# Routed pages of the last six blocks: stored whole by SyncE and gathered later, in place of a scatter by Pool

## The chip, the cores and the metric

The kernel runs on one core of a Trainium2 chip. The metric is the device time of one execution in microseconds (us); lower is better. All data are fp32 (the one-hot matrices of the routing are bf16).

## The reference

A two-layer graph network on 8192 tokens (128 graphs of 64 nodes) of width D = 256. Each layer adds a graph convolution and then a mixture of experts.

```python
# layer 0
n = layernorm(x)
h = silu(rmsnorm((eps * n + adj @ n) @ W1 + b1))         # 256 -> 1024
x = x + (h @ W2 + b2)                                    # 1024 -> 256
n = layernorm(x)
top, idx = top_k(n @ gate_w.T, 6)                        # 6 of 64 experts per token
s = softmax(top)
lattice = sum_k s[k] * (n @ lattice_weights[idx[k]])     # 256 x 256 per expert
x = x + layernorm(n + lattice @ out_w.T + out_b)
# layer 1
n = layernorm(x)
x = x + (n + relu((adj @ n) @ W_rel + b_rel + n @ W_root))
n = layernorm(x)
x = x + sum over top 2 of 8 experts of softmax weight * (relu(n @ W1[e] + b1) @ W2[e] + b2)
```

## The kernel before

The tokens are worked on in 32 blocks (NB) of 256 tokens, two tiles of 128 partitions each. There are four stages.

**The first fused pass** goes over the blocks in a software pipeline (`staggered`, a list of steps with lags, so that a step of the loop holds pieces of eight blocks or so). It computes layer 0's convolution, the gate's logits, the top six experts and each token's row in the table of that expert. Pool sends each tile's rows, six times per token, into a DRAM table `r0x` with an indirect transfer (`Router.send`, L334). A row is 258 words: 256 of the token, its target row in the answers (token x 6 + rank), and its softmax weight. `Router.places` works out the rows with 64-wide one-hot products on DVE, `Router.books` keeps the experts' chunks of the table. After the last block `Router.page_table` computes, on DVE, where each page of 128 rows starts and which expert it belongs to. The lattice weights, 16 MB, are loaded into SBUF piece by piece; the last pieces go to where this pass had its weights and scratch (L829 to L832).

**The expert pass** runs over pages. Twelve early pages, known before the table is complete, go first (`fetch_early`, `flip_early`, `apply_early`). Then come 202 pairs of pages: SP fetches a page with a row number read from the page table (L480); PE turns it (L903), ACT copies it (L905), PE multiplies it with the expert's matrix, chosen by a register (L918), DVE scales it by the softmax weights in place (L922), and Pool scatters the 128 rows to the answers `r0y` with an indirect transfer, each row to its own target (`Router.reply`, L341). `px` has 22 buffers of a pair. In the first 64 pairs ACT also issues one transfer each of a page of filler rows to the end of each expert's rows (`fill_end`, L193): a filler row's target lies outside of the answers, and its reply is dropped. More pages than the 404 run only under a condition on the number of pages (`needed`).

**The second fused pass** loads each block's six answers per token with two plain transfers of 768 KB by SP (`load_y`, L974), adds them up while turning them (`mixture`, L994), and computes out_proj, the layer norms, layer 1's convolution, its gate, and the sends of its rows (two per token) by Pool to the table `r1x`.

**The eight experts** of layer 1 run over 69 pages of 256 rows.

The order of PE, DVE and ACT is the order in which the code issues instructions (`manual_schedule`). The orders of SP's and Pool's instructions are chosen by a scheduler. Where steps share a tile or a DRAM tensor the framework adds semaphore waits; `alone` and `declare_no_dep` say which transfers need not wait for each other. The weights `lat` are one tile, so a matmul with a matrix chosen by a register waits for all loads into it.

Of the kernel before, what the change touches and what calls it, by code (L numbers as in the profile page):

```python
# [78 lines left out]
class Router:  # L79
# [15 lines left out]
    def __init__(self, tc, pool, small, dram, n, D, E, K, T, pg, S, epoch, name, R, total=None, like=None):  # L95
# [4 lines left out]
        self.pages = K * n // pg + E - 1  # L100

        self.likely_pages = K * n // pg + E // 2 + max(E // 8, 1)
        self.full_pages = -(-(K * n - E * (pg - 1)) // pg)
# [26 lines left out]
        if self.J > 1:  # L130
            self.nth = self.iota([P, self.J, E], [[1, self.J], [0, E]], 0, "nth")
            self.end, self.delta, self.alloc, self.none = (
                pool.tile([P, E], F32, name=name + x) for x in ("endrow", "delta", "alloc", "none"))
            self.used = pool.tile([P, 1], F32, name=name + "used")
            for t, v in ((self.delta, 0), (self.alloc, 1), (self.used, E), (self.none, 1)):
                nc.gpsimd.memset(t, float(v))
            nc.vector.tensor_scalar(self.end, self.base, float(S), None, op0=ALU.add)
# [3 lines left out]
        if total is None:  # L141
            self.answer = dram.tile([n * K, D], F32, name=name + "y")
            nc.gpsimd.iota(fill_to, pattern=[[0, pg // P]], base=n * K, channel_multiplier=0)
# [4 lines left out]
        self.taken = None  # L148
        self.fill(nc.sync, self.spare)
# [20 lines left out]

    def iota(self, shape, pattern, m, name):
        t = self.pool.tile(shape, F32, name=self.name + name)
        i = self.small.tile([P, 384], I32, name="iota", bufs=1)[:, :t.free_size()]
# [24 lines left out]
    def choose(self, logits):  # L198
# [7 lines left out]
        which = self.small.tile([P, T, K], F32, name=n + "which")  # L206
# [100 lines left out]
    def places(self, b, hot):  # L307
# [8 lines left out]
        nc.vector.tensor_add(place, pos, run)  # L316
        if self.J > 1:
# [30 lines left out]

    def add(self, i, x, y):
# [8 lines left out]
    def page_table(self, scratch):  # L358
# [10 lines left out]

        wide = lambda t, k, m: t.unsqueeze(k).to_broadcast([P, 4, m])  # L370
# [13 lines left out]
        v.tensor_scalar(full, cnt, 1.0 / pg, (pg - 1.0) / (2 * pg), op0=ALU.mult, op1=ALU.subtract)  # L384
        v.tensor_scalar(full, full, MAGIC, None, op0=ALU.add)
        v.tensor_scalar(full, full, -MAGIC, None, op0=ALU.add)
        v.scalar_tensor_tensor(part, full, -float(pg), cnt, op0=ALU.mult, op1=ALU.add)
        v.tensor_scalar(part, part, 0.0, None, op0=ALU.is_gt)
        if self.taken is not None:
            v.tensor_sub(full, full, self.taken)  # L390
        v.tensor_scalar(first, full, float(self.R), None, op0=ALU.min)
        v.tensor_sub(rest, full, first)
        v.tensor_tensor_scan(cum, num, self.zero, 0.0, op0=ALU.add, op1=ALU.add)
        self.total_pages = self.pool.tile([P, 1], I32, name=n + "total")
        if self.seen is None:
# [13 lines left out]
        start = small([J, 4], "pstart")  # L409
        self.tab = self.pool.tile([P, 2, 4], I32, name=n + "tab")  # L410
# [11 lines left out]
        v.scalar_tensor_tensor(nth, two, float(self.R), nth, op0=ALU.mult, op1=ALU.add)  # L422
        v.tensor_mul(le[:, :, :E], ate, wide(full, 1, E))
        v.tensor_reduce(no, le[:, :, :E], op=ALU.add, axis=AX.X)
        v.tensor_mul(no, no, three)
        v.tensor_add(nth, nth, no)
        if self.taken is not None:
            v.tensor_mul(le[:, :, :E], ate, wide(self.taken, 1, E))
            v.tensor_reduce(no, le[:, :, :E], op=ALU.add, axis=AX.X)
            v.tensor_add(nth, nth, no)  # L430
        for j in range(J):
            v.tensor_mul(le[:, :, :E], ate, wide(self.map[:, j, :], 1, E))
            v.tensor_reduce(start[:, j, :], le[:, :, :E], op=ALU.add, axis=AX.X)
        v.scalar_tensor_tensor(row, nth, float(pg), start[:, 0, :], op0=ALU.mult, op1=ALU.add)
        for j in range(1, J):
            v.tensor_sub(no, start[:, j, :], start[:, j - 1, :])
            v.scalar_tensor_tensor(no, nth, float(j * self.S // pg), no, op0=ALU.is_ge, op1=ALU.mult)
            v.tensor_add(row, row, no)
        v.tensor_scalar(no, kind, float(V), None, op0=ALU.is_lt)
        v.tensor_scalar(row, row, float(self.spare), None, op0=ALU.subtract)  # L440
        v.tensor_mul(row, row, no)
        v.tensor_scalar(self.tab[:, 0, :], row, float(self.spare), None, op0=ALU.add)
        v.tensor_scalar(self.tab[:, 1, :], exp, float(E - 1), None, op0=ALU.min)

    def fill_end(self, e):

        if e % 4 == 0:
            _, self.ends = self.nc.values_load_multi_w_load_instructions(
                self.last[0:1, e:e + 4], engines=[ENG.Activation], min_val=0, max_val=self.spare - self.pg,
                skip_runtime_bounds_check_because="the rows of an expert end in its chunk")  # L450
        self.fill(self.nc.scalar, self.ends[e % 4])

    def load(self, what, i, engine):
# [3 lines left out]
            self.tab[i // 4:i // 4 + 1, what, :], engines=[engine], min_val=0, max_val=top,  # L457
# [3 lines left out]
    def needed(self, n):  # L461

        _, (v,) = self.nc.values_load_multi_w_load_instructions(
            self.total_pages[0:1, :], min_val=0, max_val=self.pages,
# [14 lines left out]
    def fetch(self, i, row, out):  # L479
        d = self.nc.sync.dma_start(out=out, in_=self.table[ds(row, self.pg), :].rearrange("(t p) d -> p t d", p=P))  # L480
        if i < self.full_pages:
# [13 lines left out]
def two_layer_gnn_moe_kernel(ctx: ExitStack, tc: tile.TileContext, a: dict, out: bass.AP):  # L495
# [16 lines left out]
    READY = 5  # L512
    LOOK = 20
# [57 lines left out]
    def load_adjacency(b):  # L571
        at = adjacency[b % 4]
# [4 lines left out]

    x1_dram = [dram.tile([C, D], F32, name=f"x1_{b}") for b in range(NB)]
    xn1_dram = [dram.tile([C, D], F32, name=f"xn1_{b}") for b in range(NB)]
    r0 = Router(tc, const, small, dram, N, D, E0, K0, T, P, 14 * P, 4, "r0", 3)  # L580
# [23 lines left out]
    with tc.tile_pool(name="c0", bufs=1) as c0, \  # L604
# [12 lines left out]
        def load0(b):  # L617
# [3 lines left out]
            B["at"] = load_adjacency(b)  # L621
# [133 lines left out]
        def choose(b):  # L755
            B = blocks[b]
            B["top"], B["hot"] = r0.choose(pg)
# [8 lines left out]
        def place(b):  # L766
# [4 lines left out]
            if b == READY - 1:  # L771
                r0.look_back()
            if b == LOOK:
# [8 lines left out]
        def load_lattice(b):  # L782
            n = free[0] // 16
            if 8 <= b < 24:

                nc.vector.memset(lat[:1, (b - 8) * n, 0, :1], 0.0)
                nc.sync.dma_start(out=lat[:, (b - 8) * n:(b - 7) * n], in_=lat_w[:, (b - 8) * n:(b - 7) * n])

# [36 lines left out]
            (1, load_lattice),  # L825
        ))
        r0.page_table(sq.rearrange("p c n -> p (c n)"))
        n = free[0] // 16
        nc.sync.dma_start(out=lat[:, 16 * n:free[0]], in_=lat_w[:, 16 * n:free[0]])  # L829
        for i in (0, 5, 2, 3, 1, 6, 4):  # L830
            e = E0 - EB * (i + 1)
            nc.sync.dma_start(out=lat[:, e:e + EB], in_=lat_w[:, e:e + EB])  # L832
# [3 lines left out]
    with tc.tile_pool(name="e0", bufs=1, reuse_waits="tile") as ex, \  # L836
# [39 lines left out]
        staggered(EARLY // 2, ((-2, flip_early), (0, apply_early)))  # L876


    with tc.tile_pool(name="wx0", bufs=3, reuse_waits="tile") as wx, \
            tc.tile_pool(name="pt1", bufs=4, space=PSUM, reuse_waits="tile") as pt_pool, \  # L880
            tc.tile_pool(name="py1", bufs=4, space=PSUM, reuse_waits="tile") as py_pool:
        npair = (r0.pages + 1) // 2
        pairs = [dict() for _ in range(npair)]
        regs = {}
        ring = [wx.tile([P, KD, C], F32, name="pxT", bufs=5)]

        def fetch(j):
            Q = pairs[j]
            Q["px"] = px = wx.tile([P, 2, W], F32, name="px", bufs=22)
            for q in range(2):  # L890
                i = 2 * j + q
                if i % 4 == 0:
                    regs["row"] = r0.load(0, i, ENG.SP)
                if i < r0.pages:
                    r0.fetch(i, regs["row"][i % 4], px[:, q:q + 1, :])

        def flip(j):
            Q = pairs[j]
            pt = pt_pool.tile([P, KD, C], F32, name="pt")
            n = min(2, r0.pages - 2 * j)  # L900
            for q in range(n):
                for k in range(KD):
                    nc.tensor.transpose(pt[:, k, ts(q, P)], Q["px"][:, q, ts(k, P)], ident)  # L903
# [375 lines left out]
```

## Time and profile before

| | |
|---|---|
| median of 14 runs | 2308.92 us (2291.88 to 2319.18) |
| the profiled execution's own time | 2309.56 us |
| its span in the profile | 2307.8 us |
| mean granted TensorE clock | 0.948 |
| PE busy in the span | 1997.1 us, 87% |
| Pool busy | 1158.0 us, 50% |
| DVE busy | 1196.0 us, 52% |
| sends of the first pass (L334) on Pool | 384, 1039 ns each |
| replies (L341) on Pool | 404, 972 ns each |

The profile is of one execution. Busy time counts the instructions that compute, and on Pool the indirect transfers, which its processors work out themselves; transfers that SP and ACT issue are not busy time. A line of a group has the source line, the engine, the operation, output and input, the count, then busy time, mean duration in ns of one, and the idle time of that engine just before these instructions with what ended most of it. A line of waits has the waiting engine, tile and line, what it waited for, and then total us, times, and the longest. "issue" is a wait for nothing that the profile shows.

### The profile page before, as it was taken

Reading aid. Unit: us, or ns where it says so; the run is one execution under the profiler, and the core shown is the slowest. Engines: PE = TensorE matmul, PEld = TensorE weight load, DVE = VectorE, ACT = ScalarE, POOL = GpSimd, SP = SyncE. Lnnn points to the kernel's source line nnn. Section 1 sums busy time; section 2 is a strip of 40 time slices with the busy share of each in tenths; the row PEclk is TensorE's granted clock in tenths of the full one; section 3 lists DMA queues with packets and bytes.
Section 4 is the critical chain, followed back from the end, with each engine's and each line's share of the span. In section 5 each row is a group of like instructions: output and inputs, shape, how many; then the busy total and the mean of one; then the engine's idle time right before and its main releaser. Section 6 shows DMA issues by size and latency. Waiting matters only on the chain. (4 is left out here: it accounts for less than half of the span.)

```text
span 2307.8 us, 37214 instructions
## 1 busy us (share of the span) xinstructions
PE 1997.1 (87%) x10516; PEld 1714.3 (74%) x10516; DVE 1196.0 (52%) x4205; ACT 1012.8 (44%) x2033; POOL 1158.0 (50%) x1134
## 2 busy tenths in 40 slices
PE   7988888888884687887878887999997999999997
PEld 6877777777663466666766766888886888888886
DVE  5878778778786222222223224999997222222221
ACT  5867666667661121211111113666664333333332
POOL 0455555556556566666666661333334343444443
PEclk9999999999996899899998898999998999999998
DMA  3323444444345787755555527998872776676674
GB/s 110 99 100 130 138 139 136 138 139 132 106 161 186 217 244 211 220 175 171 178 175 173 154 66 276 324 318 273 277 237 78 171 173 153 166 165 165 165 165 97
DMA packets 282560, 397.91 MB, mean 172 GB/s; under 512 B 56024, under 2 KB 236392, under 8 KB 282352
## 3 DMA queue, kind: packets, MB, share of 16 engines
q1 hardware_dynamic: 202880, 246.61, 36.2%
q0 software_dynamic: 64416, 136.14, 19.8%
q10 hardware_dynamic: 15056, 12.69, 1.7%
q8 instruction: 94, 1.54, 0.3%
q14 instruction: 114, 0.93, 0.1%
HBM read 222.84 MB, written 176.64 MB: 173 GB/s over the span
## 5 line engine op out<-in xcount | busy, mean ns | idle before, releaser
L334 POOL DMA_INDIRECT r0x<-xs,r0row x384 | 398.9, 1039 | 349.1 <-DVE xs L305 145.5
L918 PE MATMUL py<-lat,pxT 128*128 x1616 | 424.5, 409 | 112.2 <-ACT pxT L905 79.6
L341 POOL DMA_INDIRECT r0y<-px x404 | 392.8, 972 | 227.6 <-DVE px L922 109.3
L918 PEld LDWEIGHTS py<-lat,pxT 128*128 128x128 f32 x1616 | 314.8, 205 | 165.8 <-ACT pxT L905 87.7
L922 DVE TENSOR_SCALAR px<-py,px 128x256 f32<-128x256 f32 x404 | 170.5, 478 | 449.4 <-PE pt L903 161.8
L351 POOL DMA_INDIRECT out_x<-py_s,px x138 | 214.7, 1556 | 292.9 <-DMA out_x<-py_s,px 211.7
L905 ACT COPY pxT<-pt 128x512 f32<-128x512 f32 x202 | 114.0, 588 | 517.2 <-remote 193.3
L1217 ACT ACTIVATE phid<-ph,pw 128x256 f32<-128x256 f32 x276 | 130.9, 474 | 322.5 <-issue 212.4
L1215 PE MATMUL ph<-pxT,pw 128*128 128x256 f32 x1104 | 251.6, 381 | 0.7 <-ACT pxT L1206 0.7
L1235 PE MATMUL py<-fw,phid 128*128 (+1 forms) x1104 | 249.7, 379 | 0.0
L717 PE MATMUL ps<-lat 128*128 128x256 f32 x1024 | 245.9, 390 | 0.0
L684 PE MATMUL ph<-lat 128*128 128x256 f32 x1024 | 239.3, 392 | 5.9 <-DVE lat L706 2.8
L1215 PEld LDWEIGHTS ph<-pxT,pw 128*128 128x128 f32 x1104 | 211.1, 191 | 30.2 <-ACT pxT L1206 1.1
L334 POOL DMA_INDIRECT r1x<-xs,r1row x128 | 127.3, 994 | 200.2 <-ACT xn3T L1106 51.9
L684 PEld LDWEIGHTS ph<-lat 128*128 128x128 f32 x1024 | 198.0, 196 | 37.2 <-issue 7.8
L1235 PEld LDWEIGHTS py<-fw,phid 128*128 128x128 f32 x1104 | 204.5, 190 | 25.0
L717 PEld LDWEIGHTS ps<-lat 128*128 128x128 f32 x1024 | 198.5, 196 | 26.6
L903 PE MATMUL pt<-ident,px 128*128 128x128 f32 x808 | 132.1, 286 | 15.5 <-DMA px<-r0x 8.2
L903 PEld LDWEIGHTS pt<-ident,px 128*128 128x128 f32 x808 | 108.0, 149 | 42.6 <-issue 19.3
L1229 DVE TENSOR_SCALAR p<-p 128x2 f32<-128x2 f32 x69 | 13.5, 195 | 228.0 <-ACT p L1228 228.0
L687 ACT ACTIVATE lat<-ph,c_L_gnn_b 128x256 f32<-128x256 f32 x256 | 101.0, 472 | 61.9 <-PE ph L684 38.5
L1238 DVE TENSOR_TENSOR py_s<-py,pb 128x512 f32<-128x512 f32 x69 | 47.7, 691 | 153.4 <-PE py L1235 153.3
(303 smaller groups left out, 2980.0 us busy)
## 6 DMA issues: line engine op xcount, KB each, us to landing
px<-r0x SPq DMA_DIRECT2D x404, 129.0 KB
y<-r0y SPq DMA_DIRECT2D x64, 768.0 KB
pw<-in_L_ffn_W1b SPq DMA_DIRECT2D x69, 514.0 KB
px<-r1x SPq DMA_DIRECT2D x69, 258.0 KB
x<-x SPq DMA_DIRECT2D x64, 256.0 KB
pb<-in_L_ffn_b SPq DMA_DIRECT2D x69, 128.0 KB
r0x<-r0filler ACTq DMA_DIRECT2D x64, 129.0 KB
lat<-in_x SPq DMA_DIRECT2D x32, 256.0 KB
```

Of the source, the lines that this page charges most:

```text
L334: i = self.nc.gpsimd.indirect_dma_start(out=self.table[:, :], out_offset=bass.IndirectOffsetOnAxis(ap=row[:, t, k:k + 1], axis=0), in_=xs[ ...
L341: d = self.nc.gpsimd.indirect_dma_start(out=self.answer[:, :], out_offset=bass.IndirectOffsetOnAxis(ap=x[:, self.D:self.D + 1].bitcast(I32 ...
L351: i, d = f"{self.name}add{i}", self.nc.gpsimd.indirect_dma_start(out=self.total[:, :], out_offset=bass.IndirectOffsetOnAxis(ap=x[:, self.D ...
L684: nc.tensor.matmul(ph[:, c, :], lhsT=w1[:, k, ts(2 * j + c, P)], rhs=B["aggT"][:, k, :], start=(k == 0), stop=(k == KD - 1))
L717: nc.tensor.matmul(B["po"][:, t, :], lhsT=B["hT"][:, c, ts(t, P)], rhs=w2[:, c, :], start=False, stop=(t == T - 1 and c == KH - 1))
L903: nc.tensor.transpose(pt[:, k, ts(q, P)], Q["px"][:, q, ts(k, P)], ident)
L905: nc.scalar.copy(xT[:, :, :n * P], pt[:, :, :n * P])
L918: nc.tensor.matmul(py[:, q, :], lhsT=xT[:, k, ts(q, P)], rhs=lat[:, ds(regs["e"][(2 * j + q) % 4], 1), k, :].rearrange("p o d -> p (o d)") ...
L922: nc.vector.tensor_scalar(px[:, q, :D], py[:, q, :], px[:, q, D + 1:D + 2], None, op0=ALU.mult)
L1215: nc.tensor.matmul(ph, lhsT=w[:, k * F1 + c * P:k * F1 + (c + 1) * P], rhs=Q["xT"][:, k, :], start=(k == 0), stop=(k == KD - 1))
L1217: nc.scalar.activation(hid[:, c, :], ph, AF.Relu, bias=w[:, KD * F1 + c:KD * F1 + c + 1], scale=1.0)
L1235: nc.tensor.matmul(py[:, t, :], lhsT=Q["hid"][:, c, ts(t, P)], rhs=fw2[:, ds(e, 1), c, :].rearrange("p o d -> p (o d)"), start=(c == 0), s ...
```

## The change

The tokens' blocks are split into the first 26 ("near") and the last six ("far", `FAR = 6`), and the pages of layer 0's experts with them:

- A page with near rows in it is a near page; a page that holds only far rows is a far page. There are two page tables: `page_table` for the near pages, and a new function `far_table`, issued on DVE after the early pages, for the far ones. The expert pass runs 168 pairs of near pages and 34 pairs of far pages, 404 pages as before; the far pairs are strewn between the near ones from the 40th item on. `px` has 20 buffers of a pair.
- Far pages have no reply on Pool. SP stores them whole, in the order of the page's rows, to a slot of a new DRAM tensor `r0paged` (`Router.store`). Near pages from number 128 on have a reply on Pool and a store on SP, since they may hold far rows too.
- `Router.clear` writes zeros to the slots that no store may reach, with 30 transfers of up to 1 MB on SP in the first fused pass.
- The far blocks keep the experts' numbers (`which`) and the places within the expert (`nth`, five more DVE operations in `places`). `Router.locate` turns them into rows of `r0paged`, with twelve DVE operations for a far block, two per item in 36 items of the expert pass, ahead of the scale.
- In the second fused pass the far blocks are worked on among the near ones (steps 7, 12, 17, 22, 27 and 31), and their answers are fetched by Pool with 12 indirect gathers of 128 rows each, four per step of the loop, instead of by `load_y`.
- The fillers of `fill_end` are issued by SP instead of ACT, three per pair for the first 22 pairs. One of the lattice loads, the last, is issued after `far_table`, whose scratch it overwrites.
- Two more conditions follow the expert pass: one runs further far pairs, one runs stores of the first 128 near pages, where the counts call for it.

The core of the diff, with the new functions:

```diff
+    def store(self, slot, y):
+        d = self.nc.sync.dma_start(out=self.paged[ts(slot, self.pg), :], in_=y)
+        self.alone(d.ins, "store")
+
+    def clear(self, lo, hi):
+        self.nc.sync.dma_start(
+            out=self.paged[lo * self.pg:hi * self.pg, :].rearrange("(s p) d -> p s d", p=P),
+            in_=self.filler[:, 0:1, :self.D].to_broadcast([P, hi - lo, self.D]))
+
+    def locate(self, b, work):
...
+        def find(what):
+            return (lambda: v.tensor_mul(prod, hot, spread(what)),
+                    lambda: v.tensor_reduce(got, prod, op=ALU.add, axis=AX.X))
+        return (
+            lambda: v.tensor_tensor(hot, spread(self.expert), self.whiches[b].unsqueeze(3).to_broadcast([P, T, K, E]),
+                                    op=ALU.is_equal),
+            *find(far),
+            lambda: v.tensor_tensor(prod[:, :, :, 0], nth, got, op=ALU.is_ge),
+            lambda: v.tensor_copy(self.whiches[b], prod[:, :, :, 0]),
+            *find(more),
+            lambda: v.tensor_mul(self.whiches[b], self.whiches[b], got),
+            *find(begin),
+            lambda: v.tensor_add(got, got, self.whiches[b]),
+            lambda: v.tensor_add(at, got, nth),
+        ), at
+
+    def gather(self, at, t, k, y):
+        self.nc.gpsimd.indirect_dma_start(
+            out=y[:, t, k, :], out_offset=None, in_=self.paged[:, :],
+            in_offset=bass.IndirectOffsetOnAxis(ap=at[:, t, k:k + 1], axis=0))
...
     def places(self, b, hot):
...
+        if self.is_far(b):
+            nth = self.nths[b] = self.pool.tile([P, T, K], F32, name=n + f"nth{b}")
+            prod = self.work.tile([P, T, K, E], F32, name=n + "prod", bufs=1)
+            nc.vector.tensor_sub(prod[:, :, 0, :], place, self.base.unsqueeze(1).to_broadcast([P, T, E]))
+            nc.vector.tensor_mul(prod[:, :, 1:, :], hot[:, :, 1:, :],
+                                 prod[:, :, 0:1, :].to_broadcast([P, T, K - 1, E]))
+            nc.vector.tensor_mul(prod[:, :, 0, :], hot[:, :, 0, :], prod[:, :, 0, :])
+            nc.vector.tensor_reduce(nth, prod, op=ALU.add, axis=AX.X)
...
     def fill_end(self, e):
...
-        self.fill(self.nc.scalar, self.ends[e % 4])
+        self.fill(self.nc.sync if self.split else self.nc.scalar, self.ends[e % 4])
...
-        r0.page_table(sq.rearrange("p c n -> p (c n)"))
+        far_table = r0.page_table(sq.rearrange("p c n -> p (c n)"))
...
-        for i in (0, 5, 2, 3, 1, 6, 4):
-            e = E0 - EB * (i + 1)
-            nc.sync.dma_start(out=lat[:, e:e + EB], in_=lat_w[:, e:e + EB])
+        load_back(0, 5, 2, 3, 1, 6)
...
         staggered(EARLY // 2, ((-2, flip_early), (0, apply_early)))
+        far_table()
+        load_back(4)
...
+            def apply(self):
+                if not self.far and not self.again:
+                    for e in range(3 * self.j, min(3 * self.j + 3, E0)):
+                        r0.fill_end(e)
...
+                for f in self.extra:
+                    f()
+                kept = self.far or self.again or self.pages[0] >= r0.sure
+                for q, i in enumerate(self.pages):
+                    nc.vector.tensor_scalar(px[:, q, :D], py[:, q, :], px[:, q, D + 1:D + 2], None, op0=ALU.mult)
+                    if not self.far and not self.again:
+                        r0.reply(i, px[:, q, :], px[:, q, :D])
+                    if kept:
+                        r0.store(i + (r0.slots[0] if self.far else 0), px[:, q, :D])
...
+            staggered(len(items), ((-12, lambda s: items[s].fetch()), (0, lambda s: items[s].apply()),
+                                   (-2, lambda s: flip(items[s], True)), (-3, lambda s: flip(items[s], False))))
...
+        for j, x in enumerate(near(0, mean_pages)):
+            items.append(x)
+            while more and j >= lead and (j - lead + 1) * mean_far >= (mean_far - len(more) + 1) * (mean_pages - lead - 2):
+                items.append(more.pop(0))
...
+        for x in items[lead + 4::2]:
+            if work:
+                x.extra = work.pop(0), *([work.pop(0)] if work else [])
...
+        with tc.If(r0.needed(2 * mean_far, r0.far_total)):
+            run(beyond(mean_far, (r0.far_pages + 1) // 2))
+        with tc.If(r0.needed(0, r0.short)):
+            run([Pair(j, again=True) for j in range(r0.sure // 2)])
...
+        def gather_y(b, lag, i):
+            if b < NB - FAR:
+                return
+            B = blocks[b]
+            if lag == 0 and i == 0:
+                B["y"] = work.tile([P, T, K0, D], F32, name="yg", bufs=1)
+            k = lag * YS + i
+            r0.gather(found[b], k // K0, k % K0, B["y"])
+
         def load_y(b):
+            if b >= NB - FAR:
+                return
...
-        staggered(NB, (
+        gathers = lambda i: tuple((m - 5, lambda b, m=m: gather_y(b, m, i)) for m in range(3))
+        steps = (
...
+        staggered(NB, tuple((lag, f if f is load_w2 else lambda s, f=f: f(order[s])) for lag, f in steps))
```

## The prediction

> **What bounds the kernel now.** I read the table of slices first, to split the span into stages.
>
> ```profile
> PE   7988888888884687887878887999997999999997
> POOL 0455555556556566666666661333334343444443
> PEclk9999999999996899899998898999998999999998
> DMA  3323444444345787755555527998872776676674
> ```
>
> One slice is 57.7 us. Slices 0 to 12 are the fused pass (to about 733 us), slices 13 to 23 the expert pass (first reply 774, last 1394), slices 24 to 30 the second fused pass (to about 1780), the rest the eight experts. The change edits the first three. Pool's digit is highest in the expert pass, 6, but not 9; PE stands at 7 to 8, so neither is full there. Next, the groups of instructions of that pass.
>
> ```profile
> L918 PE MATMUL py<-lat,pxT 128*128 x1616 | 424.5, 409 | 112.2 <-ACT pxT L905 79.6
> L341 POOL DMA_INDIRECT r0y<-px x404 | 392.8, 972 | 227.6 <-DVE px L922 109.3
> L922 DVE TENSOR_SCALAR px<-py,px 128x256 f32<-128x256 f32 x404 | 170.5, 478 | 449.4 <-PE pt L903 161.8
> L905 ACT COPY pxT<-pt 128x512 f32<-128x512 f32 x202 | 114.0, 588 | 517.2 <-remote 193.3
> ```
>
> A reply costs Pool 0.97 us and 0.30 us of issue, 1.276 us. 404 of them are 515 of the 620 us: Pool is 83% taken, and its order has no other work. Whether Pool paces this pass is the question on which the sign hangs, so I asked for the waits between 800 and 1390 us, and for those of SP.
>
> ```profile
> ACT pxT L905 <- remote: 175.3, 36, 10.5
> DVE px L922 <- PE pt L903: 161.8, 35, 8.5
> POOL r0y L341 <- DVE px L922: 105.1, 57, 2.7
> POOL r0y L341 <- issue: 103.7, 322, 1.9
> PE py L918 <- ACT pxT L905: 72.2, 30, 5.9
> ```
> ```profile
> SPq L480 <- DMA r0y<-px: 30.1, 16, 3.4
> ```
>
> Pool waits 105 us for DVE. DVE scales `px` in place, so Pool can hold up PE in one way only: a reply frees its `px` buffer late, SP fetches late, PE finds no page. SP waits for replies 30 us in all, and the fetches of pair j are issued a nearly constant 44 us ahead of its flip from pair 42 on, by the records of L480 and L903. PE never starves for a page. The pace, 2.9 to 3.1 us per pair (flips: pair 60 at 951.1, pair 180 at 1313.8), is set by PE, ACT and DVE: PE's work for a pair takes 2.17 us at full clock, and about every fifth pair a hole of 2.5 to 6 us opens in which ACT's copy and DVE's scale resume together, late (PE stands from 1090.0 to 1095.6; in the hole Pool sends three more replies and then runs dry too). The holes add up to 119 us of the 590. The trace does not name their cause. The windows show what follows from them.
>
> ```profile
> 800.00:850.00 50.00, 43.08 (x219) 36.28 (x219) 14.52 (x34) 9.96 (x17) 30.58 (x32) 0.96 0.88 259
> 1000.00:1050.00 50.00, 39.40 (x185) 33.07 (x186) 13.46 (x32) 9.28 (x17) 31.27 (x34) 0.90 0.57 174
> 1350.00:1400.00 50.00, 35.04 (x164) 29.54 (x162) 12.77 (x30) 6.84 (x12) 29.17 (x30) 0.81 0.30 99
> 1450.00:1500.00 50.00, 50.00 (x345) 45.19 (x346) 45.02 (x206) 32.38 (x69) 18.60 (x22) 1.00 0.96 327
> ```
>
> Columns are the window, its length, busy time of PE, PE weight load, DVE, ACT and Pool with counts, granted clock, DMA share, GB/s. 32 replies pass in the window with a DMA share of 0.88 as in that with 0.57: transfers do not pace the expert pass. In the second fused pass PE is full, 50 of 50, and DMA at 0.96.
>
> **The change, part by part.** The sum is made against the profiled execution, 2309.56 us (span 2307.8); the median of the runs shown is 0.64 lower.
>
> *First fused pass.* Added: 30 transfers on SP that clear some 31 MB, without a wait on compute; DMA share is 0.2 to 0.4 in slices 0 to 10, and 31 MB at the 259 GB/s of the window at 800 are 120 us of a 730 us pass, so they fit, but the first blocks' x loads stand behind some of them on SP. For the six late blocks five more DVE operations each; the two wide ones and the reduction by the rows of the same forms (768 elements, 0.95 us; 640 about 0.85), the rest 0.2: 2.4 us a block. DVE is some 80% busy in a step of 21.2 us, PE 87%, so four of six blocks' share hides. After the last block DVE alone runs `page_table`: eleven operations of 64 elements (0.20 each) and one lookup (0.42 + 0.42) more, 3.2 us, all on the path (L372 to L443 stand alone from 733 to 752.5). I take +4, between 0 and 14.
>
> *Start of the expert pass.* Now the last lattice load (L832) leaves at 752.5 and the first `py` of the main loop starts at 770.3. In the changed order the last megabyte of the lattice waits for `far_table`, which stands on DVE behind the early pages, the last of which DVE ends at 769.9. `far_table` has some 50 operations; priced as in `page_table` (0.42 for 4x64, 0.2 for the small ones, 0.56 a scan), 14.3 us: it ends at 784 or, with the longer table, 787. Then 512 KB pieces land in 3.4 us and 768 KB in 6.6, so the first `py` comes near 790 to 794, 20 to 24 later. Does it come back? Nine pairs are fetched by then, but 56 of the 64 fill transfers, now SP's, stand between the next 25 pairs' fetches. SP issued the dynamic fetches of pairs 6 to 36 at 1.9 us a pair (776 to 836), 0.95 each; a static transfer takes 0.37 to 0.50, 0.95 if it queues like those. So from 787 SP needs 25 x 1.9 = 48 and 56 x 0.4 to 0.95 = 22 to 53 us, and has pair 34 out between 857 and 888. PE, at the old 2.9 us a pair from 792, comes to it near 890: at the worse price just fed, and in no case faster than it was. Nothing comes back. +20, between 8 and 30.
>
> *Replies to stores.* 68 far pages lose their reply: Pool is relieved of 68 x 1.276 = 87 us. By the waits above that frees an engine that waits, so I take 0, between -87 (if Pool were the bound) and 0. Added: 276 stores of 128 KB on SP. From 888 on SP has 168 pairs x 1.9 = 319 us of fetches and 276 x 0.5 to 0.6 = 138 to 166 of stores, and would end near 1345 to 1373; PE, started 20 late at the old pace, fetches its last page near 1355. So SP, idle before, becomes level with PE. But each store waits for a DVE scale, and the next fetches stand behind that wait on SP; with 18 pairs of lead that is covered by some 53 us, less when SP falls back. SP also shows stretches in which each of its instructions takes 0.7 us. I take +5; at 0.95 us a store the stores are 262 us, SP ends at 1469, about 100 late. The 35 MB on the DMA engines are +0.9 us a pair beside 1.7 now, under a pace of 3.0: free. Here the Trainium skill speaks against the idea: its page "DMA: Bandwidth & Descriptors", section "Issuing engines are not separate DMA queues", says that transfers from all issuing engines run on the same 16 DMA engines, and that spreading the issue saves only the sequencer's time. The trace agrees that the sixteen are shared (0.88 at 800 with fills, fetches and replies together), and shows that they do not pace this stage; by the rule alone the swap would gain nothing and cost the added bytes.
>
> *Locating.* 72 DVE operations, seven of 0.95 and five of 0.17 per block, 45 us in all, two per pair on 36 pairs. DVE is busy 13.5 of 50 us here; a step of 3 us has room, but they stand before the scale, so each delays PSUM's release by up to 1.9 us, covered by four `py` buffers. +2, between 0 and 15.
>
> *Tail of the pass.* Two more conditions on every engine. An If costs ACT 1.0 us now (1381.2 to 1382.2), PE 3.7. The stores must land before the far gathers; +3, between 1 and 8. No branch of the three should run: the counts of these inputs stay under their thresholds (335 near pages for 336, 65 far for 68).
>
> *Second fused pass.* 72 gathers of Pool replace 12 of the 64 y loads. Pool's step has four sends, 5.7 us of about 10.9; four gathers at 1.28 make 10.8 in 18 of 32 steps: level with PE. The gathers stand in front of the sends on Pool, whose wait at the end is short. Against this stage's DMA share of 0.96 the bytes are the same. +5, between 0 and 25.
>
> Sum: 4 + 20 + 5 + 0 + 2 + 3 + 5 = +39, so 2348.
>
> **The rivals.** *Pool paces the expert pass after all.* For it: Pool's period, 2.55 us a pair, is above PE's 2.17, its idle time is spread thin, and when PE holds fast Pool's queue grows; the holes of ACT and DVE might come with Pool's descriptor work. Against it: the waits. Then up to 87 us go, and the costs of 39 stay: 2261, between 2255 and 2300. It decides if the pace falls below 2.7 us a pair in the stretch of far pairs. *SP becomes the bound*: stores at 0.95 us, pass three starts near 1469 instead of 1389: +80 and the costs outside, about 2400. It decides if an SP step of two fetches and 1.64 stores passes 3.0 us. *The start is made good and the rest hides*: 2309, no change. *A branch runs*: 34 pairs x 2.95 = +100; the inputs' counts speak against it.
>
> A second rule bears on the holes. After PE stands from 1117.5 to 1123.7 the granted clock is 0.50 for some 4 us: a hole costs more than its length. "TensorE: Matmul & The Clock Gate", section "What's actually happening", has the clock halved after an idle window; fewer holes would thus pay twice, in the rival's favour, which no row here can settle.
>
> **How the numbers follow.** My forecast 0.44, SP as the bound 0.18, Pool as the bound 0.27, all hidden 0.08, a branch 0.03. About 0.3%, 7 us, is what a measurement of this kernel can tell from no change: faster 0.27, same 0.08, slower 0.65. The likeliest case alone runs from 2322 to 2385. The range reaches into both neighbours, to 2262 (most of the Pool case kept) and to 2400, and leaves out half of SP's tail and the branch.
>
> **What would show it.** Right: the first main `py` 15 to 25 us later than 770; pairs at 2.9 to 3.1 us all through the far stretch; Pool's waits for DVE grown by about 87 us; the second fused pass about 390 us as now. Wrong: pairs under 2.7 us after item 40 (Pool did pace), or over 3.2 with SP's queue full and PE waiting on `px` (SP paces); a second fused pass above 410 us with PE waiting on gathered y; a first `py` before 780.

## The result: 5% slower

The changed kernel takes 2434.37 us (median of ten runs), the kernel before 2308.76 us (47 runs): a ratio of 1.054, between 1.051 and 1.057. The profiled execution has a span of 2430.6 us, 122.8 us more than the one before. The experiments below are single executions, each beside one of the kernel before; that took 2306 to 2326 us in the series e1 to e4, e9 to e12 and e13 to e16, but 2057 us in the series e5 to e8, on the chip of e1 to e4 (the other two series ran on two more chips), so that those four are compared with 2057 and with each other alone.

The page of the changed kernel, slices of 60.8 us:

```profile
PE   7988888888843779978778829788889899999997
POOL 0456555556564556655444421444453434444444
PEclk9999999999976889999999969888889899999999
DMA  9964444443363777777777768766763476776665
```

The clearing shows in DMA's first three slices and does not touch PE there. PE's expert pass has two parts, 9 9 7 and then 8 7 7 8. The hole at its end (2) is deeper than before, and the second fused pass, which was 9 throughout, is full of 8. Its groups:

```profile
L370 POOL DMA_INDIRECT r0y<-px x336 | 335.5, 999 | 288.7 <-DVE px L1099 194.8
L1092 PE MATMUL py<-lat,pxT 128*128 x1616 | 411.8, 400 | 52.6 <-issue 21.7
L1099 DVE TENSOR_SCALAR px<-py,px 128x256 f32<-128x256 f32 x404 | 174.1, 479 | 398.4 <-PE py L1092 212.3
L1082 ACT COPY pxT<-pt 128x512 f32<-128x512 f32 x202 | 115.3, 587 | 525.2 <-PE pt L1080 292.3
```

Pool waits for DVE 195 us now (109 before): grown by 86, near the 87 that the prediction named as a sign. By first and last instructions of each stage:

| stretch | before, us | after, us | difference | predicted |
|---|---|---|---|---|
| start to the end of `page_table` | 752.5 | 763.0 | +10.5 | +4 |
| to the first `py` of a pair | 17.8 | 34.9 | +17.1 | +20 |
| to the end of the last scale | 619.6 | 601.8 | -17.8 | +7 |
| to the first transpose of the mixture | 3.9 | 36.3 | +32.4 | +3 |
| to the first matmul of the eight experts | 388.8 | 471.9 | +83.1 | +5 |
| to the end | 525.2 | 522.7 | -2.5 | 0 |

The expert pass got faster and the two stretches behind it, priced at 8 us together, cost 115. The first row varies from run to run where the code is the same (749 to 800 us in the runs of the changed kernel's kind below).

Windows of the three parts of the expert pass (length, busy PE, weight load, DVE, ACT, Pool; clock, DMA share, GB/s), then two lines of the waits from 1040 to 1400 us, of PE and of Pool:

```profile
900.00:1040.00 140.00, 128.10 (x671) 110.14 (x670) 74.23 (x157) 31.20 (x56) 90.64 (x90) 0.96 0.70 210
1040.00:1390.00 350.00, 279.98 (x1322) 216.91 (x1322) 110.46 (x248) 63.80 (x110) 176.06 (x178) 0.96 0.74 229
1390.00:1436.00 46.00, 8.80 (x45) 7.42 (x44) 4.35 (x10) 1.17 (x2) 11.28 (x13) 0.65 0.53 176
```
```profile
POOL r0y L370 <- DVE px L1099: 128.9, 51, 6.6
...
PE pt L1080 <- DMA px<-r0x: 45.5, 49, 2.6
```

From item 36 to 90 an item takes 2.52 us (904.8 to 1040.9) and PE is busy 128 of 140 us. From item 96 the fetches' lead over the flips, up to 13 us until then, is 1 to 3 us, PE waits for `px` 45.5 us (8.2 in the whole kernel before), and an item takes 3.2 us. From 1040 to 1390 SP issues 216 fetches and 214 stores: the slots of the stores' transfers sum to 97 us, 0.45 each, and those of the fetches with their moves, waits and register loads to 244 us, 1.13 each. SP's own waits from 1040 to 1400 are small beside that, some 34 us in all; the two largest:

```profile
SPq L620 <- DMA r0paged<-px: 17.2, 20, 2.5
SPq L380 <- DVE px L1099: 14.0, 38, 1.6
```

So SP is all but full, and its fetches come just in time or late.

The end of the pass in the timeline (start, duration of a row of like instructions, engine, line):

```profile
1396.02 22.20 SPq L380 DMA_DIRECT2D r0paged<-px  x30
...
1402.29 0.98 POOL L370 DMA_INDIRECT r0y<-px  x1 [0.30 <-issue]
...
1431.25 5.42 SPq L1200 DMA_DIRECT2D y<-r0y  x3
...
1436.03 1.30 PE L1220 MATMUL ps<-ident,y 128*128 128x128 f32 x5 [37.23 <-DMA y<-r0y]
```

SP has 30 stores left and issues the last at 1418, 18 us after the last scale. Then no engine computes and no transfer is issued for 13 us, until 1431; before, the first y load left at 1389.1, ahead of the end of the last scale. By SP's records these 13 us are its three conditions, one of which the kernel before has too. From each branch to SP's next instruction it takes 2.49, 2.70 and 2.72 us (from 1418.8, 1422.4 and 1427.8). The queue that loads instructions moves six packets of 8 KB from 1418.3 to 1431 (packets, MB, share):

```profile
q14 instruction: 6, 0.05, 1.2%
```

In the second fused pass 26 of 31 steps take about 11 us as before, and five take 22.8 to 29.6: those in which Pool gathers for a far block (the gathers for the first of the six stand at the start of the pass). Two windows on either side of one, then the timeline inside it:

```profile
1500.00:1520.00 20.00, 20.00 (x131) 17.77 (x130) 16.79 (x78) 13.37 (x29) 8.67 (x10) 1.00 0.96 329
1520.00:1540.00 20.00, 5.34 (x28) 2.94 (x26) 4.52 (x21) 0.84 (x2) 13.41 (x15) 0.66 0.57 180
```
```profile
1514.18 1.03 POOL L419 DMA_INDIRECT yg<-r0paged,r0at  x1 [3.19 <-issue]
...
1518.32 2.82 PE L1220 MATMUL ps<-ident,y 128*128 128x128 f32 x24
...
1520.97 0.60 PE L76 MATMUL ps<-ident,hn 128*128 128x128 f32 x4
...
1524.71 0.15 DVE L316 TENSOR_TENSOR xs<-r1top 128x1 f32<-128x1 f32 x1
...
1532.29 0.95 POOL L419 DMA_INDIRECT yg<-r0paged,r0at  x1 [0.30 <-issue]
...
1536.43 0.98 POOL L363 DMA_INDIRECT r1x<-xs,r1row  x1 [0.30 <-issue]
1538.24 0.81 SPq L1200 DMA_DIRECT2D y<-r0y  x2
1538.24 0.58 ACT L1223 COPY accT<-ps 128x512 f32<-128x512 f32 x1 [18.91 <-remote]
```

Pool issues transfer after transfer from 1514 to 1537, with hardly a pause. PE's mixture (L1220) is through by 1521.1, but its signal, which ACT's copy and SP's next y load wait for, counts only at 1538.22, after the run: SP, DVE and ACT stand for 16 to 19 us, and PE, which has other work at first, for 12. The profile models the ends of matmuls, so it does not tell whether the last matmul or only its signal was late. This is the picture of the holes in the expert pass before, three times as long (in the one at 1090 PE's signal counts 4.6 us late). Pool's order also is not four gathers a step: the scheduler set all twelve of a block among some five sends.

### The profile page after: what moved, and what is told of

Read it like the earlier page. It is cut to its first block, busy times and chain, and to the rows that moved or that the text cites. A ratio compares the mean times of both kernels' runs of the same rounds, so it can differ in the third digit from the quotient of the medians.

```text
span 2430.6 us, 37876 instructions
## 1 busy us (share of the span) xinstructions
PE 2031.0 (84%) x10516; PEld 1717.8 (71%) x10516; DVE 1271.3 (52%) x4366; ACT 1013.5 (42%) x2033; POOL 1174.5 (48%) x1142
## 5 line engine op out<-in xcount | busy, mean ns | idle before, releaser
L370 POOL DMA_INDIRECT r0y<-px x336 | 335.5, 999 | 288.7 <-DVE px L1099 194.8
L1092 PE MATMUL py<-lat,pxT 128*128 x1616 | 411.8, 400 | 52.6 <-issue 21.7
L1092 PEld LDWEIGHTS py<-lat,pxT 128*128 128x128 f32 x1616 | 307.1, 200 | 104.0 <-issue 47.6
L1082 ACT COPY pxT<-pt 128x512 f32<-128x512 f32 x202 | 115.3, 587 | 525.2 <-PE pt L1080 292.3
L1080 PE MATMUL pt<-ident,px 128*128 128x128 f32 x808 | 139.0, 285 | 74.5 <-DMA px<-r0x 65.2
L1080 PEld LDWEIGHTS pt<-ident,px 128*128 128x128 f32 x808 | 100.2, 145 | 121.4 <-issue 52.0
L851 DVE SCALAR_TENSOR_TENSOR lat<-ph,c_L_gnn_b,rms 128x256 f32<-128x256 f32 x256 | 103.1, 475 | 51.9 <-ACT rms L59 33.8
```

The lines of the kernel that those rows point to most:

```text
L370: d = self.nc.gpsimd.indirect_dma_start(out=self.answer[:, :], out_offset=bass.IndirectOffsetOnAxis(ap=x[:, self.D:self.D + 1].bitcast(I32 ...
L1080: nc.tensor.transpose(pt[:, k, ts(q, P)], self.px[:, q, ts(k, P)], ident)
L1082: nc.scalar.copy(xT[:, :, :n * P], pt[:, :, :n * P])
L1092: nc.tensor.matmul(py[:, q, :], lhsT=self.xT[:, k, ts(q, P)], rhs=lat[:, ds(e, 1), k, :].rearrange("p o d -> p (o d)"), start=(k == 0), st ...
```

## The experiments

**The gathers.** e1 takes them out; e14 and e5 halve them; e10 and e6 spread them.

```diff
 def gather_y(b, lag, i):
-    if b < NB - FAR:
-        return
+    return
...
 def load_y(b):
-    if b >= NB - FAR:
-        return
...
-    in_=r0.answer[ts(b * T + t, P * K0), :]
+    in_=r0.answer[ts((b if b < NB - FAR else b - 20) * T + t, P * K0), :]
```

> The changed kernel, but the far blocks' answers are read by plain loads of SP (the answers of another block, so the values are not the reference's), and Pool gathers nothing. The order of the blocks stays. Theory A, each burst of twelve gathers stops the other engines: the second fused pass goes from 472 us (1436 to 1908) to about 390, the steps are 11.0 us without the five of 23 to 30 us, the kernel takes about 2350 us. Rival B, the new order of the blocks or late loads make the long steps: they stay, the pass stays above 450 us, the kernel above 2420.

2331.9 us. The second fused pass takes 388.0 us, with no long step: theory A. The order of the blocks costs nothing.

```diff
-    r0.gather(found[b], k // K0, k % K0, B["y"])
+    if k < K0:
+        r0.gather(found[b], k // K0, k % K0, B["y"])
+    elif k == K0:
+        nc.sync.dma_start(out=B["y"][:, 1], in_=...)   # plain, 768 KB
```

> The changed kernel with six gathers and one plain load for each far block, as before. Theory A, the stop goes with the length of Pool's unbroken run: the second fused pass 390 to 415 us where the changed kernel has 472. Rival B, with the number of transfers: half of the 83 us, 425 to 435. Rival C, a fixed stop for each block: above 455.

2377.5 us. The pass takes 416.6 us: +28 for half of the gathers where all cost +83. The five steps are 14.2 to 18.6 us, 3 to 8 too long where they were 12 to 19. Half of the gathers cost a third: 416.6 lies between the ranges, 2 us above A's and 8 below B's. e5 is the same kernel in the series with the kernel before at 2057:

> The changed kernel, but only the first tile of a far block is gathered by Pool (six gathers in place of twelve); the second is one plain load of SP (another block's answers). Theory A, the other engines are stopped for as long as Pool's unbroken run of gathers and sends lasts beyond what is queued: the five long steps shrink by more than half, from 23 to 30 us to 11 to 17, the second fused pass from 472 to 390 to 415 us. Rival B, each far block costs the same stop, whatever the number of gathers (a wait for the stores, or for the buffer): the five steps stay near 25 us, the pass above 455 us.

It took 2191.4 us, the pass 410.6, within A's range; the long steps are 13 to 18 us.

```diff
-    YS = 4
+    YS = 3
...
-    r0.gather(found[b], k // K0, k % K0, B["y"])
+    at = work.tile([P, 1], I32, name="yat", bufs=12)
+    nc.vector.tensor_copy(at, found[b][:, k // K0, k % K0:k % K0 + 1])
+    nc.gpsimd.indirect_dma_start(out=B["y"][:, k // K0, k % K0, :], ..., ap=at, axis=0)
...
-gathers = ... (m - 5, ...) for m in range(3)
+gathers = ... (m - 6, ...) for m in range(4)
```

> The 72 gathers spread three per step over four steps, as before. Theory A, it is the unbroken run on Pool that stops the others: second fused pass 390 to 410 us where the kernel before has 389, against 472 of the change. Rival B, the number of indirect transfers sets it, however they are spread: above 455 us where the kernel before has 389.

2433.2 us beside 2459.2 of the changed kernel in the same series (e9). The pass takes 446.8 us where the changed kernel has 473.8: between A and B. No step is over 17.5 us, but most are 12 to 14 instead of 11.0. So spreading saves 27 of 85 us; 72 spread gathers still cost 58, 0.8 us each, as 36 in shorter runs do. Both the number and the unbroken run count. e6 has the same edit in the series where the kernel before takes 2057 us:

> The changed kernel with all 72 gathers, but spread: three per step over four steps, each held to its place by a copy of its index column on DVE, so that Pool's order has a send of layer 1 after each gather in place of runs of up to five gathers. Theory A, it is the unbroken run on Pool that stops the others: the long steps go, the second fused pass takes 390 to 410 us, the kernel 2350 to 2375. Rival B, the number of indirect transfers sets it, however they are spread: the pass still loses 15 us per far block, above 455 us.

2181.6 us, the pass 406.5, within A's range; there halving and spreading come out alike (410.6 and 406.5), each some 25 us over the 383 us of e7, which gathers nothing.

> The changed kernel as it is, beside the next three, since in the last call the kernel before took 2057 us on the same chip where it had taken 2316 in the call before, with the same program. If the kernel before is at 2300 to 2320 here, the changed one is at 2412 to 2446; if it is at 2057, the holes are gone, the relief of Pool is worth nothing and the costs alone show: SP as the bound of the second half of the expert pass, the start, the conditions, the gathers, together 120 to 170 us, so 2180 to 2230.

2459.2 us beside 2325.8: the first case, 13 us above its range.

**SP's issue.** e2 moves the stores to ACT.

```diff
-    d = self.nc.sync.dma_start(out=self.paged[ts(slot, self.pg), :], in_=y)
-    self.alone(d.ins, "store")
+    self.nc.scalar.dma_start(out=self.paged[ts(slot, self.pg), :], in_=y)
```

> The changed kernel with the stores issued by ACT instead of SP. Theory A, SP's issue of two fetches and 1.7 stores per item sets the 3.2 us of the items from the 90th on: they fall to 2.5 to 2.7 us, the last scale comes near 1340 instead of 1400, the store tail after it (18 us) shrinks, the kernel takes 2355 to 2375 us. Rival B, the added 35 MB on the shared DMA engines set the pace: still 3.1 to 3.3 us an item, 2425 to 2440. Rival C, ACT's waits for the scale hold its next copy back: over 3.3 us an item and slower than 2440.

2368.6 us, theory A: 2.2 to 2.8 us an item from item 48 to the end, last scale at 1352.9, first mixture 17.8 us later instead of 36.3. From item 60 on the fetches are again issued 29 to 38 us ahead of their flips, and PE waits for no `px` from 1040 to 1340 (38 us in the changed kernel). So SP's issue was the bound, and not the stored bytes: a window of e2 has a DMA share of 0.88, with PE busy 43 of 50 us (39 of 50 in the kernel before at 1000 to 1050):

```profile
1100.00:1150.00 50.00, 43.04 (x234) 37.01 (x233) 19.00 (x43) 11.14 (x19) 29.90 (x30) 1.00 0.88 279
```

**The two conditions.** e3 leaves them out, e15 keeps them with short bodies.

```diff
 with tc.If(r0.needed(2 * mean_far, r0.far_total)):
-    run(beyond(mean_far, (r0.far_pages + 1) // 2))
+    nc.sync.dma_start(out=wait, in_=r0.paged[0:1, 0:4])
 with tc.If(r0.needed(0, r0.short)):
-    run([Pair(j, again=True) for j in range(r0.sure // 2)])
+    nc.sync.dma_start(out=wait, in_=r0.paged[0:1, 0:4])
```

> The changed kernel without the two added conditions after the expert pass (neither branch is taken with these inputs, so the output is the same). Theory A, the conditions cost most of the 13 us between the last store's issue and the first y load: the kernel is 6 to 12 us faster, about 2425. Rival B, they hide behind the stores that still have to land: no more than 2 us, 2432 to 2436.

2410.7 us: faster by more than expected. From the last scale to the mixture it takes 23.6 us in place of 36.3. By the spans 9 us more are gone, 5 in the first pass and 4 in the second fused pass, where the code is the same: that is within what these stages vary by.

> The changed kernel with the two added conditions, but each with a body of one small transfer in place of 33 and 64 pairs (not taken either). Theory A, jumping over the long bodies costs the 13 us: as without the conditions, about 12 us less from the last scale to the first mixture than the change's 36. Rival B, a condition costs its register load and branch on every engine, whatever the body: 34 to 36 us as now.

2409.6 us, theory A: 22.2 us in place of 36.3, as without the conditions. What costs is to jump over the long bodies, 34 and 64 pairs by the code. From SP's last store to its first y load the changed kernel takes 13.0 us and e15 4.0: a short body is jumped in 0.2 us, while the old condition, whose body is 20 pairs, still takes 2.6. So the jumps with what SP does at each of them are 9 of the 14 us; the other 5 are stores that were out sooner (13.3 us after the last scale instead of 18.5), and no run tells why.

The Trainium skill names a mechanism in "Runtime: NRT & Kernel Launch", section "Instruction fetch mechanics": a taken branch whose target is outside the two fetched pages makes the engine wait for a load of the target page. The traces agree: the changed kernel moves six packets of 8 KB on the instruction queue in its 13 us of three long jumps, and e15 two in its one long jump and none in the short ones.

**What the replies cost.** Four runs on the kernel before; in each the answers are cleared in the first pass by 48 transfers, and those not replied stay zero. e4 omits every second pair's replies, e11 and e7 replace all replies of pairs by ACT's plain stores, e13 by Pool's plain stores.

```diff
+    if j % 2 == 0:                                                    # e4
         r0.reply(2 * j + q, px[:, q, :], px[:, q, :D])
...
-    r0.reply(2 * j + q, px[:, q, :], px[:, q, :D])
+    nc.scalar.dma_start(out=junk[ts(2 * j + q, P), :], in_=px[:, q, :D])   # e7, e11; Pool's in e13
```

> The kernel before, with the replies of every second pair left out (the answers are cleared in the first pass instead with 48 transfers of 1 MB, so half of them stay zero). Theory A, the replies set the pace, 1.55 us for each with all that they hold up: pairs fall from 3.0 to 2.2 to 2.5 us, the expert pass from 620 to 450 to 510 us, the kernel to 2140 to 2200. Rival B, PE, ACT and DVE set the pace without Pool, as the prediction had it: pairs stay at 2.9 to 3.1 us, the kernel at 2300 to 2320.

2144.6 us beside 2316.1. Theory A, and stronger: from pair 24 on every pair takes 2.17 us, PE's own work, without a hole:

```profile
1000.00:1050.00 50.00, 50.00 (x278) 44.10 (x278) 20.33 (x48) 13.59 (x24) 21.80 (x23) 1.00 0.62 183
```

> The kernel before with ACT's plain stores in place of all replies of the pairs, as before. Theory A, Pool's own working out of indirect transfers holds the engines up: pairs at 2.2 to 2.5 us, the expert pass 450 to 510 us, also where the kernel before has 620. Rival B, the written bytes do it: 2.8 us a pair or more there.

2190.0 us beside 2325.8, theory A: 2.17 us from pair 84 on (2.2 to 3.5 before that; ACT also issues the fillers in the first 64 pairs), with the same bytes and a higher DMA share:

```profile
1000.00:1050.00 50.00, 50.00 (x279) 44.09 (x278) 20.16 (x46) 13.70 (x24) 0.00 (x0) 1.00 0.86 244
```

e7 is the same kernel in the other series:

> The kernel before, with each of the 404 replies of the pairs replaced by a plain store of the page by ACT to a scratch tensor (the answers are cleared in the first pass, as in the run with half of the replies, and stay zero beyond the early pages). The bytes written stay the same; Pool has nothing to do in the expert pass. Theory A, Pool's own working out of indirect transfers is what holds the engines up: pairs at 2.2 to 2.4 us, the expert pass 450 to 490 us, the kernel 2120 to 2190. Rival B, the written bytes and their traffic on the DMA engines do it: pairs at 2.8 us or more, the kernel above 2260.

2071.2 us, below its range for A; its expert pass, 475 us by the scales, is within it. But the kernel before took 2057 there: without holes there was nothing to gain.

> The kernel before, with each of the 404 replies of the pairs replaced by a plain store of the page, issued by Pool, to a scratch tensor (the answers are cleared in the first pass). Theory A, any transfer whose descriptors Pool works out holds the others up: pairs stay at 2.8 us or more where the kernel before has 3.0, the kernel above 2260. Rival B, it is the scatter of 128 rows by an index: pairs at 2.17 to 2.5 us, the kernel 2140 to 2200 where the kernel before has 2310.

2135.4 us beside 2306.2, rival B: 2.17 us from pair 24 on, though Pool issues 404 transfers still. Its group and a window:

```profile
L930 POOL DMA_DIRECT2D junk<-px x404 | 216.1, 540 | 229.9 <-DVE px L929 193.4
```
```profile
1000.00:1050.00 50.00, 50.00 (x279) 44.06 (x278) 20.16 (x46) 13.46 (x23) 23.33 (x45) 1.00 0.79 241
```

A plain transfer takes Pool 0.54 us, a scatter 0.97. Pool is busy 47% here, 44% in e4, and 61 to 66% in the windows of the kernel before from 800 to 1350 us. So the written bytes are cleared, and Pool's transfers as such. Whether it is the working out of the index, the scattered rows that it writes to, or that Pool is never idle for long, these runs do not separate.

**Repairs together.** e8 and e12 have ACT's stores and spread gathers, and compute the whole reference; e16 has ACT's stores, e1's plain loads and no conditions.

> The changed kernel with both repairs: stores issued by ACT, and gathers spread three per step. If the two causes are separate, their gains add: expert pass as with ACT's stores (last scale near 1353), second fused pass 390 to 410 us, the kernel 2285 to 2310, level with the kernel before or just ahead of it. If Pool's work only moves, one of the stages gives it back: above 2340.

2134.3 us beside 2057: the holes were absent, so the expected time did not apply; the pass takes 410.3 us, as expected. The difference to e6, 47 us, is that of ACT's stores.

> Both repairs, ACT's stores and spread gathers, as before. If the two causes are separate: last scale near 1353 and a second fused pass of 390 to 410 us where the kernel before has 389, in all 2285 to 2310 beside 2310 of the kernel before; where the kernel before takes 2057, again near 2134.

2393.8 us beside 2325.8 and e9's 2459.2, far above the 2285 to 2310 expected. The expert pass kept its gain, from 604 to 563 us by the scales, but the gathers cost as much as in e10 (a pass of 445.1 us where 390 to 410 was expected), and the first pass, whose code is the same, ended 23 us later than in e9. The repaired kernel is ahead of the change and still behind the kernel before.

> The changed kernel with stores issued by ACT, the far blocks' answers by plain loads (of another block's answers) and without the two conditions. If the costs found so far are separate, 102 + 66 + 24 us go: 2235 to 2260 where the change takes 2434 and the kernel before 2310, so that the relief of Pool shows as 50 to 75 us. If the items stay at 2.65 us because the remaining replies hold PE up, the last scale comes near 1350 as with ACT's stores alone.

2293.9 us beside 2306.2, above the 2235 to 2260 expected. The expected sum of 192 us came from differences of whole executions; by the stages the three costs are 81 us in the second fused pass, 26 in the tail and 36 in the expert pass. The scales take 562 us from first to last where the kernel before has 616: the relief of Pool, with ACT's stores in the same pass, is worth 54 us. The items still take 2.3 to 3.0 us from the 48th on; whether the 336 replies that are left hold them there, or ACT's stores between its copies, no run separates (e8, in the other series, has 2.3 to 2.6 in its second half). The start, 30 us later, takes more than half of the 54 back. Even without gathers, conditions and SP's stores 12 us are left, which is less than single executions of the kernel before differ by (2292 to 2324), and no version that computes the reference beats the kernel before.

## Why the prediction was wrong

The sign was right, and the range, to 2400, too low. Against the sum of +39 the spans differ by +123. The second fused pass is 78 us above its term and the tail 29; the expert pass is 25 below. Its signs of being wrong came: pairs under 2.7 us after item 40 (2.52, up to item 90), then SP full with PE waiting on `px` (at 3.2 us an item), and a second fused pass above 410 us. By its steps:

- *First pass and start*, +24 against +28: near, though the first pass's part, +10, is within what that stage varies by. `far_table` ends at 784.6, as priced, but the late lattice load leaves SP only at 792.0, behind fetches of pairs, and the first `py` comes at 797.9. By item 36 the flips are 31 us late: nothing came back.
- *Replies to stores, relief of 0*: wrong. It read "Pool waits for DVE" as slack. Pool did not hold PE through the ring of `px`, as I said; but with Pool's indirect transfers PE's signals come late, and the holes that I gave to PE, ACT and DVE go when these are halved (e4) or replaced (e11, e13). The trace before shows the picture: in the holes at 1090, 1181, 1236 and 1290 ACT resumes 1.1 us after the end of a run of ten replies, which I took for Pool running dry. The rival *Pool paces* had the right cause, with -87 for what e16 shows as -54.

```profile
1092.89 0.97 POOL L341 DMA_INDIRECT r0y<-px  x1 [0.30 <-issue]
...
1094.96 0.59 ACT L905 COPY pxT<-pt 128x512 f32<-128x512 f32 x1 [10.46 <-remote]
```

- *Replies to stores, SP at +5*: wrong, and the second rival had it. The stores cost a little less than I took (0.45 us, not 0.5 to 0.6), but the fetches 1.13 us, waits included, instead of 0.95, and PE had become faster than SP. From about item 90 SP is the bound; by e16's 562 against the change's 598 that took back 36 us. That this stretch ended within 25 us of the forecast is luck: it is the difference of two missed terms, -54 and +36.
- *Tail*, +3 against +32: wrong. I had SP ending level with PE, and priced the conditions by what one costs ACT and PE. But SP ends 18 us late with its stores and then goes through its jumps, 2.5 to 2.7 us each, before it can load y. Short bodies take 14 us off (e15), ACT's stores 18.5 (e2).
- *Second fused pass*, +5 (up to 25) against +83: the largest miss. I let a full Pool delay Pool's own sends only; e1 shows the gathers to cost all of it, and the trace PE's signal 17 us late with SP, DVE and ACT standing. And I took four gathers per step from the code, where the order of Pool, which a scheduler sets, has a block's twelve close together; spreading them is worth 27.
- *Locating* and the rule on shared DMA engines: nothing speaks against them, and no run tests the locating alone. The rule's conclusion, that spreading the issue saves only the sequencer's time, is what e2 measures: 43 us of the expert pass, because a sequencer was the bound.

## What to carry to other kernels

An engine that "waits for" another may still be what slows it. Before pricing a relief at nothing, take half of its work away and look: one run of that kind turned a pass of 3.0 us a pair into one of 2.17. Work moved to a later stage takes its cost along: 68 replies became 72 gathers, at 0.8 to 1.2 us each. And the jump over code that never runs has a price, which counts in full on the engine that is late.

## What the runs showed of the hardware

- A run of Pool's indirect transfers holds back other engines. PE's signal at the end of a mixture came 17 us late, with ACT, SP and DVE standing; SP's instructions (from 1087 to 1095 us in the kernel before) and PE's (from 1522 to 1525 in the changed one) go by at 0.7 us each in such stretches. The trace shows no cause behind it, and which shared part is blocked stays open.
- This is not always so. In one series, on a chip where the kernel before had taken 2316 us, it took 2057. In e5 and e6 the items from 36 to 108 ran at 2.17 us with all near replies in place, and in all four runs the first pass, with its 384 sends on Pool, ended at 650 to 653 us where the other runs have 749 to 801. The SP-bound half of the pass (2.9 to 3.3 us an item) and a cost of the gathers (about 25 us, halved or spread) remained, and the eight experts took as long. What differed there, nothing here shows. The change itself was not run in that series; e6, with spread gathers, is 124 us behind 2057.
- A jump over an untaken body takes SP 2.5 to 2.7 us with bodies of 20, 34 and 64 pairs, without growing with their length, and 0.2 us with a body of one transfer. The two added conditions with their long bodies cost 13 to 14 us from the last scale to the mixture.
